# One rotating pool of four PSUM banks for all small TensorE outputs of a four-layer graph attention kernel

## The chip, the cores and the metric

The kernel runs on one core of a Trainium2 chip. The metric is the device time of one execution in microseconds: three runs of the kernel before gave 2642.32, 2642.26 and 2640.95, the median is 2642.26. The profile is one more execution, taken by the hardware profiler; its span is 2639.2 us. Five engines take part: TensorE (PE; its weight loads have a row of their own, PEld), VectorE (DVE), ScalarE (ACT), GpSimd (POOL) and SyncE (SP), which only issues transfers here. Each engine works through its own list of instructions in order, and waits at semaphores for the others.

## What is computed

Sixteen graphs of 1024 nodes with 256 features go through four graph attention layers. All share one adjacency matrix. Layers 0 and 2 have four heads of 64 features, layers 1 and 3 one head of 256. The reference, cut to one layer:

```python
h = jnp.maximum(_layernorm(x, axis=-1), 0.0)
Wh = (h @ W).reshape(B, N, H, D)
e = s_src[:, :, None, :] + s_dst[:, None, :, :]      # two dot products of Wh with a
e = jnp.where(e > 0, e, slope * e)
e = jnp.where(mask, e, -jnp.inf)
alpha = jax.nn.softmax(e, axis=2)
h_out = jnp.einsum('bijh,bjhd->bihd', alpha, Wh)
x = x + jax.nn.elu(h_out)                            # relu in layer 3
```

All inputs and outputs are float32.

## The kernel before

**Steps.** One step is one layer of one graph: 64 steps in all. `order_of_steps` interleaves four graphs ("streams"), so that the next layer of a graph is prepared while steps of other graphs run.

**A step's main part.** `weights` (L335, DVE) makes the unnormalised attention tile `w` of 128 source nodes by 1024 target nodes; there are 18 buffers for such tiles. `aggregate` (L351, PE) multiplies `w` with the projected features `whx` and accumulates over the eight source tiles in a PSUM tile `acc`: for four heads one `acc` holds four target tiles of one head (128 x 260), for one head it holds one target tile (128 x 257). ScalarE copies every `acc` to SBUF (L366). An `acc` tile is done with when this copy has read it.

**A step's ending.** `finish` divides by the softmax sum and applies ELU on DVE, ACT and POOL (L383, L392, L399, L405, L406): only then is the graph's new `x` there.

**The preparation of a later step.** `preparation` takes the statistics of `x` (L222 on DVE, L245 to L257 on POOL), normalises on ACT (`xn`, L263), transposes on PE (L271) and applies ReLU on the way out of PSUM (`hT`, L272). It projects each of the eight node tiles on PE (L282, 128 x 264 or 128 x 258) and copies the result to SBUF on ACT (L284); after every fourth projection two short exponentials follow on ACT (L290, L292), and after the last one two more (`factors`, L300 and L301). `rows` transposes the attention factors on PE (L306), ACT copies them (`gT`, L308), and a transfer through DRAM spreads them over the partitions (`gs`, L324), whence ACT puts them into PSUM (`g`, L330).

**The order.** The order on each engine is the order in which Python emits the pieces: `tc.manual_schedule()` takes it as it is. Between two calls of `aggregate`, `prepare` emits those pieces of later steps whose hand-written due times (`FOUR`, `ONE`, `LATE`, in eighths of a step) have come. So runs of transposes and projections stand between aggregations on PE, and their copies stand in the same order on ACT, between the copies of `acc`.

**PSUM.** [...] `ps_g` holds two tiles of two banks for `g`. `ps_acc` has two banks, for `acc` (and for half of the mask transposes at the start). `ps_p` has two banks, named `pp`, for transposes, projections, rows, and two small things done four times in all (L132, L152). A tile taken from a pool gets a buffer that an earlier tile has left; the first matmul into it waits until the last reader of that earlier tile is through.

Of the kernel before, what the change touches and what calls it, by code (L numbers as in the profile page):

```python
# [14 lines left out]

# [1 line left out]

# [6 lines left out]
F32 = mybir.dt.float32  # L26
BF16 = mybir.dt.bfloat16
# [5 lines left out]
PSUM = bass.MemoryType.PSUM  # L33

P = 128
# [25 lines left out]
def kernel(ctx: ExitStack, tc: tile.TileContext, x, adj, ws, avs, out):  # L61
    nc = tc.nc
    B, N, F = x.shape
    C = N // P
    K = F // P
    HALF = C // 2
# [27 lines left out]
    small = ctx.enter_context(tc.tile_pool(name="small", bufs=4))  # L94
    work = ctx.enter_context(tc.tile_pool(name="work", bufs=2))
    ps_g = ctx.enter_context(tc.tile_pool(name="ps_g", bufs=2, space=PSUM))
    ps_acc = ctx.enter_context(tc.tile_pool(name="ps_acc", bufs=2, space=PSUM))
    dram = ctx.enter_context(tc.tile_pool(name="dram", bufs=4, space=bass.MemoryType.DRAM))
    ps_p = ctx.enter_context(tc.tile_pool(name="ps_p", bufs=2, space=PSUM))

    L = len(LAYERS)
    steps = order_of_steps(B, L)
    xs = {}
    state = [dict() for _ in steps]

    def heads_of(t, H):


        return t[..., 0:F + H].rearrange("p c (h d) -> p c h d", h=H)
# [7 lines left out]
    def weight_columns(l):  # L117

        H, slope, hs, _ = LAYERS[l]
        D = F // H  # L120
        st = {}

        def vectors(queue=nc.sync):

            st["a"] = prep.tile([P, HALF, H, D], F32, name="e")
            queue.dma_start(
                out=st["a"][0:1, 2:4],
                in_=bass.AP(tensor=avs[l].tensor, offset=avs[l].offset,
                            ap=[[0, 1], [D, 2], [hs, H], [1, D]]))

        def spread():
            pa = ps_p.tile([P, 2, H, D], F32, name="pp")  # L132
            nc.tensor.matmul(pa.rearrange("p t h d -> p (t h d)"), lhsT=ones[0:1, :],
                             rhs=st["a"][0:1, 2:4].rearrange("p t h d -> p (t h d)"),
                             start=True, stop=True)
            nc.scalar.activation(st["a"][:, 0:2], pa, AF.Copy)

        def columns():
            for k in range(K):
                for part in range(2):  # L140
                    prod = st["a"][:, 2 + part]
                    wk = heads_of(wx[l], H)[:, k]
                    nc.vector.tensor_mul(prod, wk[:, :, 0:D], st["a"][:, part])
                    nc.vector.tensor_reduce(
                        wk[:, :, D] if part else wx[l][:, k, F + H:F + 2 * H], prod, AX.X, ALU.add)
            st["sq"] = small.tile([P, K, H], F32, name="sq", bufs=1)
            wd = heads_of(wx[l], H)[:, :, :, D]
            nc.vector.tensor_tensor(st["sq"], wd, wd, op=ALU.mult)

        def bound():  # L150

            pn = ps_p.tile([P, H], F32, name="pp")  # L152
            for k in range(K):
                nc.tensor.matmul(pn, lhsT=ones, rhs=st["sq"][:, k, :], start=(k == 0),
                                 stop=(k == K - 1))
            top = small.tile([P, 1], F32, name="top", bufs=1)
            nc.vector.tensor_reduce(top, pn, AX.X, ALU.max)
            nc.gpsimd.tensor_tensor(top, top, half1, op=ALU.pow)
            nc.gpsimd.tensor_scalar(cbias[l], top, 16.01, None, op0=ALU.mult)
            nc.gpsimd.tensor_scalar(nbias[l], top, -16.01 * slope, None, op0=ALU.mult)  # L160
            nc.gpsimd.tensor_scalar(rbias[l], top, -16.01 * (1.0 - slope), SHIFT,
                                    op0=ALU.mult, op1=ALU.add)

        return vectors, spread, columns, bound

    pairs = {}

    def mask_rows(c):

        st = {}  # L170

        def fetch_rows():
            st["raw"] = work.tile([P, N], I32, name="w", bufs=WBUFS)
            nc.sync.dma_start(out=st["raw"], in_=adj.rearrange("(p c) j -> p c j", p=P)[:, c])

        def sign():
            st["sgn"] = work.tile([P, 2, N], BF16, name="w", bufs=WBUFS)
            nc.vector.tensor_scalar(st["sgn"][:, 0], st["raw"], -1.0, 1.0, op0=ALU.max,
                                    op1=ALU.min)

        def turn():

            if c < HALF:
                if c % 2 == 0:
                    pairs[c // 2] = ps_g.tile([P, 2, C, P], BF16, name="g")
                pm = pairs[c // 2][:, c % 2]
            else:
                pm = ps_acc.tile([P, C, P], BF16, name="acc")
            st["pm"] = pm
            sgn = st["sgn"][:, 0].rearrange("p (q c) -> p c q", c=C)  # L190
            for jc in range(C):
                nc.tensor.transpose(pm[:, jc, :], sgn[:, jc, :], identb)

        def positive():
            nc.vector.tensor_scalar(masks[0][:, :, c * P:(c + 1) * P], st["pm"], 0.0, None,
                                    op0=ALU.is_gt)

        def nonzero():
            nc.scalar.activation(masks[1][:, :, c * P:(c + 1) * P], st["pm"], AF.Square)

        return fetch_rows, sign, turn, positive, nonzero

    def load(b, parts=1):
# [6 lines left out]
    def preparation(n):  # L210

        b, l = steps[n]
        H, slope, _, _ = LAYERS[l]
        D = F // H
# [51 lines left out]
        def transpose(half, k):  # L266
            if k == 0:
                st["hT", half] = prep.tile([P, K, HALF * P], F32, name="hT")
            pt = ps_p.tile([P, HALF, P], F32, name="pp")
            for q in range(HALF):  # L270
                nc.tensor.transpose(pt[:, q, :], st["xn", half][:, q, k * P:(k + 1) * P], ident)  # L271
            nc.scalar.activation(st["hT", half][:, k, :], pt.rearrange("p q i -> p (q i)"),  # L272
                                 AF.Relu)

        def project(c):
            if c == 0:
                st["whx"] = prep.tile([P, C, F + 2 * H], F32, name="whx", bufs=3)
                st["rcol"] = small.tile([P, C, H], F32, name="rcol")
            half, q = divmod(c, HALF)
            pw = ps_p.tile([P, F + 2 * H], F32, name="pp")  # L280
            for k in range(K):
                nc.tensor.matmul(pw, lhsT=st["hT", half][:, k, q * P:(q + 1) * P],  # L282
                                 rhs=wx[l][:, k, :], start=(k == 0), stop=(k == K - 1))
            nc.scalar.activation(st["whx"][:, c, :], pw, AF.Copy)  # L284
            if q < HALF - 1:
                return

            s = slice(half * HALF, (half + 1) * HALF)
            wh = heads_of(st["whx"], H)[:, s]
            nc.scalar.activation(st["rcol"][:, s], wh[:, :, :, D], AF.Exp, bias=rbias[l],  # L290
                                 scale=1.0 - slope)
            nc.scalar.activation(wh[:, :, :, D], wh[:, :, :, D], AF.Exp, bias=nbias[l],  # L292
                                 scale=slope)
            nc.gpsimd.tensor_tensor(wh[:, :, :, 0:D], wh[:, :, :, 0:D],  # L294
                                    wh[:, :, :, D:D + 1].to_broadcast([P, HALF, H, D]),
                                    op=ALU.mult)
# [5 lines left out]

        def rows():

            pt = ps_p.tile([C * H, P], F32, name="pp")
            nc.tensor.transpose(pt, st["gcol"].rearrange("p c h -> p (c h)"), ident)  # L306
            gT = small.tile([C * H, P], F32, name="gT", bufs=2)
            nc.scalar.activation(gT, pt, AF.Copy)  # L308
            st["grow"] = dram.tile([H, C, P], F32, name="grow")
            nc.sync.dma_start(out=st["grow"].rearrange("h c i -> c h i"), in_=gT)  # L310

        out = [lambda: stats(0), lambda: stats(1), combine_all, lambda: normalise(0), lambda: normalise(1)]
        for half in range(2):
            out += [lambda half=half, k=k: transpose(half, k) for k in range(K)]
            out += [lambda c=c: project(c) for c in range(half * HALF, (half + 1) * HALF)]


        out += [factors, rows, lambda: fetch_heads(n + 1), lambda: None]
        return [(at, piece) for at, piece in zip(agenda_of[n], out, strict=True)]

# [18 lines left out]
    def aggregate(n, h, i0, per):  # L339
        H = LAYERS[steps[n][1]][0]  # L340
        D = F // H
        st = state[n]
        if h == 0 and i0 == 0:
            st["y"] = work.tile([P, C, H, D + 1], F32, name="y")
        acc = ps_acc.tile([P, per, D + 1], F32, name="acc")
        cols = P // 2 if H > 1 else P
        for q in range(per):
            for jc in range(C):
# [259 lines left out]
```

## Time and profile before

| engine | busy us | share of the span | instructions |
|---|---|---|---|
| PE | 2539.8 | 96% | 40088 |
| PEld | 2256.5 | 86% | 40088 |
| DVE | 2041.7 | 77% | 2144 |
| ACT | 1133.4 | 43% | 2502 |
| POOL | 1021.5 | 39% | 1040 |

The granted TensorE clock was 0.989 of full speed on average. The share of busy time is a mean over the whole span. A PE row in the profile begins with a matmul and ends where the matmul's end is modelled, so two neighbouring rows can overlap: 16 projections take 3.73 us as a row that begins at 1193.83, and the next row begins at 1197.48, only 3.65 us later. The distances between starts are therefore the better clock for PE. In a wait list, "PE pp L282 <- ACT whx L284: 11.2, 27, 3.7" means that the PE matmuls of line 282 were preceded by 11.2 us of idle PE, 27 times, at most 3.7 us at once, and that an ACT instruction of line 284 ended it.

### The profile page before, as it was taken

What the parts mean: (1) busy time and instruction counts of PE and PEld (TensorE: products, weight loads), DVE (VectorE), ACT (ScalarE), POOL (GpSimd) and SP (SyncE); (2) the same over time, 40 slices, a digit from 0 to 9 for tenths busy, and PEclk for the clock granted to TensorE, in tenths of its full rate; (3) what the DMA queues carried; (4) which work ended last, traced back from release to release, by engine and by line L of the source; (5) the groups of instructions that cost most, each with busy time, mean ns of one, the idle gap of its engine ahead of it and who ended that gap; (6) DMA issues with size and microseconds to landing.
All of it is one profiled execution on the core that took longest, in us unless ns stands there. A gap on an engine that the chain in (4) does not pass through costs nothing.

```text
span 2639.2 us, 87794 instructions
## 1 busy us (share of the span) xinstructions
PE 2539.8 (96%) x40088; PEld 2256.5 (86%) x40088; DVE 2041.7 (77%) x2144; ACT 1133.4 (43%) x2502; POOL 1021.5 (39%) x1040
## 2 busy tenths in 40 slices
PE   6899998999999999999999999999999999999899
PEld 4788887888888888888898888888888888888888
DVE  7888566877778877778877778877778877777973
ACT  4343443344444344544344444344444344443341
POOL 2234353423433434443323444433433334444231
PEclk8999999999999999999999999999999999999999
DMA  4101001111112100102211101101112200111101
GB/s 176 51 27 42 26 26 34 42 49 67 50 58 74 42 19 34 42 34 74 74 54 62 42 34 42 42 20 65 50 58 74 74 19 34 42 34 43 51 18 56
DMA packets 36987, 128.98 MB, mean 49 GB/s; under 512 B 6278, under 2 KB 9094, under 8 KB 34696
## 3 DMA queue, kind: packets, MB, share of 16 engines
q1 hardware_dynamic: 36606, 123.36, 13.3%
q8 instruction: 314, 5.14, 0.8%
q14 instruction: 57, 0.47, 0.1%
q10 hardware_dynamic: 10, 0.00, 0.0%
HBM read 105.91 MB, written 17.43 MB: 47 GB/s over the span
## 4 chain that ended last, share of the span: by engine, by line
PE 66%; DVE 17%; POOL 7%; ACT 6%; issue 3%; DMA 0%; DVEq 0%; ACTq 0%
PE acc L351 46%; PE pp L282 15%; DVE w L335 10%; PE pp L271 4%; POOL x L406 3%; DVE e L405 3%; DVE bn L222 2%; ACT xn L263 2%; POOL rstd L251 2%; ACT e L399 1%; DVE e L392 1%; ACT whx L284 1%; ACT rcol L290 0%; ACT gcol L301 0%; ACT whx L292 0%
## 5 line engine op out<-in xcount | busy, mean ns | idle before, releaser
L351 PE MATMUL acc<-whx,w 128*64 128x65 f32 x36864 | 1911.6, 241 | 26.0 <-DVE w L335 20.9
L351 PEld LDWEIGHTS acc<-whx,w 128*64 128x64 f32 x36864 | 1747.2, 145 | 171.6 <-issue 31.2
L335 DVE SCALAR_TENSOR_TENSOR w<-g,rcol,mask 128x1024 f32<-128x1024 f32 x1280 | 1540.6, 1273 | 445.5 <-PE acc L351 387.4
L366 ACT ACTIVATE y<-acc 128x260 f32<-128x260 f32 (+1 forms) x504 | 194.4, 386 | 1097.5 <-PE acc L351 1097.5
L294 POOL TENSOR_TENSOR whx<-whx 128x1024 f32<-128x1024 f32 x128 | 256.4, 2003 | 667.1 <-ACT whx L292 667.1
L282 PE MATMUL pp<-wx,hT 128*128 128x264 f32 (+1 forms) x2048 | 488.6, 390 | 18.8 <-ACT whx L284 11.2
L393 POOL TENSOR_TENSOR y<-y,r 128x1024 f32<-128x1024 f32 x126 | 264.3, 2108 | 618.7 <-DVE e L392 490.8
L282 PEld LDWEIGHTS pp<-wx,hT 128*128 128x128 f32 x2048 | 379.6, 191 | 98.7 <-ACT whx L284 23.5
L406 POOL TENSOR_TENSOR x<-x,e 128x1024 f32<-128x1024 f32 x96 | 238.1, 2486 | 161.0 <-DVE e L405 155.5
L263 ACT ACTIVATE xn<-x,shift,rstd 128x256 f32<-128x256 f32 x512 | 261.3, 590 | 87.9 <-POOL shift L257 85.8
L284 ACT ACTIVATE whx<-pp 128x264 f32<-128x264 f32 (+1 forms) x512 | 195.7, 386 | 236.4 <-PE pp L282 236.1
L222 DVE BATCH_NORM_STATS2 bn<-x 128x6 f32<-128x256 f32 x512 | 175.8, 410 | 58.0 <-POOL x L406 54.6
L405 DVE SCALAR_TENSOR_TENSOR e<-e,y 128x1024 f32<-128x1024 f32 x96 | 175.6, 1839 | 41.7 <-ACT e L399 35.5
L271 PE MATMUL pp<-ident,xn 128*128 128x128 f32 x1024 | 168.6, 284 | 32.1 <-ACT xn L263 28.4
L271 PEld LDWEIGHTS pp<-ident,xn 128*128 128x128 f32 x1024 | 119.3, 141 | 83.2 <-ACT xn L263 53.6
L330 ACT ACTIVATE g<-gs 128x1024 f32<-128x1024 f32 x160 | 163.6, 1024 | 8.1 <-DVE w L335 4.1
L272 ACT ACTIVATE hT<-pp 128x512 f32<-128x512 f32 x256 | 136.8, 585 | 1.9 <-PE pp L271 0.5
L251 POOL TENSOR_TENSOR rstd<-rstd,neghalf 128x8 f32<-128x8 f32 (+1 forms) x65 | 107.0, 1647 | 12.6 <-DVE shift L252 7.6
L399 ACT ACTIVATE e<-e 128x1024 f32<-128x1024 f32 x96 | 100.7, 1049 | 23.9 <-DVE e L392 20.0
L392 DVE SCALAR_TENSOR_TENSOR e<-y,r 128x1024 f32<-128x1024 f32 x64 | 75.5, 1221 | 2.2
L408 DVE SCALAR_TENSOR_TENSOR x<-y,x 128x1024 f32<-128x1024 f32 x30 | 43.3, 1444 | 10.0 <-POOL y L393 10.0
L245 POOL TENSOR_TENSOR dev<-bn 128x8 f32<-128x8 f32 x63 | 13.2, 209 | 89.8 <-DVE bn L222 89.8
(63 smaller groups left out, 401.7 us busy)
## 6 DMA issues: line engine op xcount, KB each, us to landing
gs<-grow SPq DMA_DIRECT2D x160, 512.0 KB
x<-in_x SPq DMA_DIRECT2D x15, 1024.0 KB
out<-x SPq DMA_DIRECT2D x30, 512.0 KB
w<-in_adj SPq DMA_DIRECT2D x8, 512.0 KB
x<-in_x SPq DMA_DIRECT2D x2, 512.0 KB
wx<-in_L_gnn_W SPq DMA_DIRECT2D x8, 128.0 KB
out<-x SPq DMA_DIRECT2D x8, 128.0 KB
grow<-gT SPq DMA_DIRECT2D x32, 16.0 KB
```

Of the source, the lines that this page charges most:

```text
L222: nc.vector.bn_stats(bn[:, c, :], xs[b][:, c, :])
L263: nc.scalar.activation(xn[:, q, :], xs[b][:, c, :], AF.Identity, bias=st["shift"][:, c:c + 1], scale=st["rstd"][:, c:c + 1])
L271: nc.tensor.transpose(pt[:, q, :], st["xn", half][:, q, k * P:(k + 1) * P], ident)
L282: nc.tensor.matmul(pw, lhsT=st["hT", half][:, k, q * P:(q + 1) * P], rhs=wx[l][:, k, :], start=(k == 0), stop=(k == K - 1))
L284: nc.scalar.activation(st["whx"][:, c, :], pw, AF.Copy)
L294: nc.gpsimd.tensor_tensor(wh[:, :, :, 0:D], wh[:, :, :, 0:D], wh[:, :, :, D:D + 1].to_broadcast([P, HALF, H, D]), op=ALU.mult)
L335: nc.vector.scalar_tensor_tensor(w, state[n]["g", h], state[n]["rcol"][:, jc, h:h + 1], masks[LAYERS[steps[n][1]][3]][:, jc, :], op0=ALU.m ...
L351: nc.tensor.matmul(acc[o % P:o % P + cols, q, :], lhsT=st["w", h, jc][:, o:o + cols], rhs=st["whx"][:, jc, h * (D + 1):(h + 1) * (D + 1)], ...
L366: nc.scalar.activation(st["y"][:, i0:i0 + per, h, :], acc, AF.Copy)
L393: nc.gpsimd.tensor_tensor(yh, yh, rb, op=ALU.mult)
L405: nc.vector.scalar_tensor_tensor(e, e, -1.0, yh, op0=ALU.add, op1=ALU.max)
L406: nc.gpsimd.tensor_add(xh, xh, e)
```

## The change

The two pools `ps_acc` and `ps_p`, of two banks each, become one pool `ps` of four banks. Everything that used them takes its tile from there under one name. A helper, `bank`, cuts the wanted shape out of a full bank. No instruction, shape or order of pieces is edited. The purpose is that any kind of tile can use any of the four banks, so that PE can be further ahead of the engines that empty them.

```diff
-    ps_acc = ctx.enter_context(tc.tile_pool(name="ps_acc", bufs=2, space=PSUM))
+    ps = ctx.enter_context(tc.tile_pool(name="ps", bufs=4, space=PSUM))
-    ps_p = ctx.enter_context(tc.tile_pool(name="ps_p", bufs=2, space=PSUM))
...
+    def bank(*shape):
+        t = ps.tile([P, 512], F32, name="bank")
+        n = math.prod(shape)
+        if len(shape) == 1:
+            return t[:, 0:n]
...
-            pa = ps_p.tile([P, 2, H, D], F32, name="pp")
+            pa = bank(2, H, D)
...
-            pn = ps_p.tile([P, H], F32, name="pp")
+            pn = bank(H)
...
-                pm = ps_acc.tile([P, C, P], BF16, name="acc")
+                pm = ps.tile([P, C, P], BF16, name="bank")
...
-            pt = ps_p.tile([P, HALF, P], F32, name="pp")
+            pt = bank(HALF, P)
...
-            pw = ps_p.tile([P, F + 2 * H], F32, name="pp")
+            pw = bank(F + 2 * H)
...
-            pt = ps_p.tile([C * H, P], F32, name="pp")
+            pt = bank(P)[0:C * H]
...
-        acc = ps_acc.tile([P, per, D + 1], F32, name="acc")
+        acc = bank(per, D + 1)
```

More of the change, by code (lines that the diff above doesn't have):

```diff
@@ L18 @@
+import math
 from contextlib import ExitStack
@@ L104 @@
     state = [dict() for _ in steps]
+    def bank(*shape):
[3 more added lines that the diff above has]
+            return t[:, 0:n]
+        names = "abc"[:len(shape)]
+        return t[:, 0:n].rearrange(f"p ({' '.join(names)}) -> p {' '.join(names)}",
+                                   **dict(zip(names, shape)))
     def heads_of(t, H):
```

## The prediction

> **What bounds the kernel now.** I read the busy shares first, then the waits of PE and of its weight loads, then the chain of waits and the timelines of a few cycles. PE is busy 96% of the span, DVE 77%. The chain that ended last is two thirds PE:
>
> ```profile
> PE 66%; DVE 17%; POOL 7%; ACT 6%; issue 3%; DMA 0%; DVEq 0%; ACTq 0%
> ```
>
> The rest is one recurring detour. From about 340 to 2400 us the kernel repeats itself every 79.1 us (two steps; stretches 1001.91 to 1081.09, 1081.09 to 1160.26 and 1160.26 to 1239.32 are 79.18, 79.17 and 79.06 long). In each cycle the chain leaves PE once, for the ending of a step (L405 on DVE, L406 on POOL, statistics, xn on ACT), and comes back at the transposes of line 271. So a cycle is PE-bound for about 64 us, and latency-bound for about 15.
>
> In the PE-bound part, which waits are waits for a bank? A projection or transpose that waits for ACT whx, ACT gT or ACT y waits for a copy out of PSUM whose result it doesn't use: that is a bank. One that waits for ACT xn waits for data. The PE wait list, then that of the weight loads (us in total, times, longest us):
>
> ```profile
> PE pp L271 <- ACT xn L263: 28.4, 77, 8.4
> PE acc L351 <- DVE w L335: 20.9, 25, 5.2
> PE pp L282 <- ACT whx L284: 11.2, 27, 3.7
> PE pp L282 <- ACT gT L308: 7.3, 15, 0.6
> ...
> PE acc L351 <- ACT y L366: 1.0, 1, 1.0
> ```
> ```profile
> PEld pp L282 <- ACT whx L284: 23.5, 30, 4.1
> ...
> PEld pp L271 <- ACT whx L284: 17.5, 63, 0.3
> PEld pp L282 <- ACT gT L308: 13.6, 15, 1.0
> ```
>
> Bank waits are 11.2 + 7.3 + 1.0 = 19.5 us of idle PE, but 23.5 + 17.5 + 13.6 = 54.6 us (with 2.2 more at acc, 56.8) of idle weight loads. The truth lies between, and starts tell it. The PE timeline of one cycle:
>
> ```profile
> 1009.48 1.29 PE L271 MATMUL pp<-ident,xn 128*128 128x128 f32 x8
> 1010.61 3.64 PE L351 MATMUL acc<-whx,w 128*128 128x257 f32 x16
> 1014.08 1.03 PE L271 MATMUL pp<-ident,xn 128*128 128x128 f32 x8
> 1015.05 3.95 PE L351 MATMUL acc<-whx,w 128*64 128x65 f32 x128
> 1018.93 5.54 PE L282 MATMUL pp<-wx,hT 128*128 128x258 f32 x24
> 1024.64 2.05 PE L282 MATMUL pp<-wx,hT 128*128 128x264 f32 x8 [0.17 <-ACT whx L284]
> 1026.52 1.30 PE L271 MATMUL pp<-ident,xn 128*128 128x128 f32 x8
> ```
>
> The same eight transposes show 1.29 and 1.30 us after projections, but 1.03 after an accumulation. The page calls PE busy there; 0.26 us is lost each time.
>
> [...] rows overlap their successors (3.73 us long, next start after 3.65), which is how a stall stays hidden in a busy row. [...] the 63 + 30 + 15 waits above show where two are short. [...]
>
> **The change, part by part.** In the two built programs the lists of DVE, ACT, POOL and SP are the same, instruction for instruction, with waits for the same engines. PE's list has the same matmuls in the same order; only its waits differ. Before, 676 of 1352 reuses of a bank come after two tiles and 271 after three. After, 1338 of 1352 come after exactly four.
>
> *Can four shared banks be worse than two and two?* Among any five tiles in a row, three are of one kind, so under the old rule the first of these must be emptied before the last begins. Evacuations come in the order of the tiles (ACT is in order), so the oldest of the five is empty then too. The new rule asks for nothing earlier, save where DVE reads a tile too (the masks at the start, line 157, the last step). I laid the new assignment over the old times: every tile's new predecessor had been emptied at least 0.58 us before the tile began, in the steady cycles at least 1.31 us. Before, the margin at a stall is 0.05. So the added waits (an accumulator now also waits for a projection's copy, with all of PE queued behind it, and DVE waiting for PE to release w) should already be met when they are reached.
>
> *What is removed,* start to start:
> - (a) Second transpose tile after projections: 1009.48 to 1010.61 is 1.13 us for eight transposes; the chain of waits gives the unstalled eight at 1014 as 0.87. Loss 0.26, times 63: 16.4.
> - (b) Third 264-column projection, held while ACT runs L290, L292, L300, L301: 1018.93 to 1026.52 is 7.59 for eight tiles. Unstalled, four tiles take 3.65 (1193.83 to 1197.48) and 3.49 (768.57 to 772.06). Loss 0.45, times 26: 11.7.
> - (c) Second projection after rows, held by gT behind a 1.05 us exponential (L399): 1035.48 to 1039.88 is 4.40 against 3.65, loss 0.75, times 15: 11.3.
> - (d) Two long stalls at 166 and 2497 us: 3.27 and 3.74 idle, 7.5 with the restart.
> - (e) One accumulator at 425 us: 1.2.
>
> Sum 48.1.
>
> *What of it counts.* The latency-bound part starts from DVE, which runs without a real gap from 1030.93 to 1067.5, and began when PE released a w buffer:
>
> ```profile
> 1030.93 7.24 DVE L335 SCALAR_TENSOR_TENSOR w<-g,rcol,mask 128x1024 f32<-128x1024 f32 x6 [10.00 <-PE acc L351]
> ...
> 1043.07 16.77 DVE L335 SCALAR_TENSOR_TENSOR w<-g,rcol,mask 128x1024 f32<-128x1024 f32 x14 [0.21 <-PE acc L351]
> ...
> 1067.50 3.29 DVE L405 SCALAR_TENSOR_TENSOR e<-e,y 128x1024 f32<-128x1024 f32 x1 [0.22 <-ACT e L399]
> ```
>
> Both (a) and (b) lie before that release, so they shorten the whole cycle: 2 x 0.26 + 0.45 = 0.97, times 26 cycles: 25.2. Stall (c), at 1037, lies beside this DVE stretch. Of its 0.75 only the two waits inside it, 0.21 + 0.22 = 0.43, can be saved; the rest returns as a longer wait for xn. Times 14 steady cycles: 6.0. In (d), PE gets two projections further (2 x 0.87 = 1.75) and then meets the same late ACT: 2 x 1.75 = 3.5. (e) is whole: 1.2. Outside the cycles remain 11 x 0.26 and one (c), 3.6; DVE ends several waits there, so I take half: 1.8. Sum 37.7.
>
> *What is added:* 32 semaphore instructions on PE, 31 of them at the transposes. The source view has such rows at 51 ns, so 0 to 1.6 us; many stand where PE waits for xn anyway. I take 0.8. Moving a matmul to another bank costs nothing that a row shows: the copies stay 386 ns.
>
> 2642.3 - 37.7 + 0.8 = 2605.
>
> **The rivals.**
> - *All 48.1 us are saved:* DVE is not co-critical, (c) and (d) count whole. 2642.3 - 48.1 = 2594. Against it: the 0.21 and 0.22 above.
> - *The xn wait takes the place:* PE already waits 28.4 us for xn, and if DVE's start hangs on something else than PE, the detour keeps its place in time. Half of the gain stays: 2642.3 - 19 = 2623. Against it: DVE waits 10.00 us for PE right before that stretch.
> - *Slower:* the copies on ACT come in bursts (xn takes 4.05 us in one piece), and a shared pool lets one late copy stop accumulations too. If the margins were an illusion and each of 30 cycles had two new stalls like (a), with nothing gained: 2642.3 + 30 x 0.52 + 1.6 = 2660. Against it: the argument with five tiles, and margins over 1.3 us.
>
> **Chances.** Forecast 0.70, all saved 0.11, half 0.12, nothing 0.02, slower 0.05. The forecast itself is open by some 10 us (how much of (c), (d) and the edges counts). The range from 2590 to 2624 holds it and both neighbours for the most part. Faster by over 0.2%: 0.93; within 0.2%: 0.02; slower: 0.05.
>
> **What would show it.** Right: no PE or PEld wait at L282 and L271 (their new line numbers are 10 higher) for whx or gT worth over 5 us in all; all runs of eight transposes 1.03 us long unless they wait for xn; cycles of about 78.2 us without, and 77.8 with, a gT stall before; the xn wait of PE grown by some 5 us; DVE, ACT and POOL busy times unchanged. Wrong: the same waits under another name (ACT y, say), or cycles that stay at 79.1 us with a longer wait for xn, or a wait of PE for DVE w in the cycles.

## The result and the profile after

| kernel | median us | of the kernel before | 95% interval |
|---|---|---|---|
| before (4 runs) | 2641.61 | | |
| one pool of four banks (4 runs) | 2597.71 | 0.9836 | 0.9819 to 0.9853 |

The kernel before has one run more here than in the text above, 2639.95. The forecast was 2605, with a range from 2590 to 2624; the kernel came out 7 us below the forecast. PE is now busy for 2509.0 us instead of 2539.8, though it runs the same 40088 matmuls. Of the 30.8 us that went, 26.6 went at transposes (168.6 to 155.9 us) and projections (492.8 to 478.9): stalls drawn as busy rows. The rest went mostly at the accumulations; the clock was at half for 51.2 us instead of 60.9, which shortens rows too (at 273 us, 100 matmuls took 4.71 us with most of them at half clock before, and 3.14 at full clock after). Idle PE fell from 99.4 to 87.0 us, only 12.4 of the 43.2 us of shorter span.

The wait list of PE after the change (lines stand 10 higher than before):

```profile
PE bank L281 <- ACT xn L273: 32.3, 92, 9.7
PE bank L361 <- DVE w L345: 21.4, 24, 5.2
...
PE bank L361 <- ACT whx L294: 3.0, 1, 3.0
...
PE bank L292 <- ACT whx L294: 1.8, 1, 1.8
```

Of the bank waits (11.2 for whx, 7.3 for gT, 1.0 for y) two single ones are left, 4.8 us together. The wait for xn, which is data, grew from 28.4 to 32.3.

The list of the weight loads wants care. Before:

```profile
PEld acc L351 <- issue: 31.2, 115, 1.0
```

After:

```profile
PEld bank L361 <- issue: 15.6, 50, 1.7
PEld bank L361 <- ACT whx L294: 13.7, 31, 3.4
...
PEld bank L361 <- ACT rcol L300: 5.5, 33, 0.2
```

This looks like a new bank wait at the accumulators. It is mostly an old gap with a new name. When tiles of 128 columns are followed by tiles of 64, the first weight load waits 0.17 us after transposes and 0.35 after projections, in either kernel. An accumulator now carries a wait for a projection's copy, and the profile puts the gap down to it. Starts show that nothing was added: from the last transpose to the first matmul of 64 columns it is 203 ns before and 202 after, 94 more than between two transposes (109).

The PE timeline of the same piece of a cycle as in the prediction:

```profile
1001.80 7.32 PE L292 MATMUL bank<-wx,hT 128*128 128x258 f32 x32
1008.96 1.04 PE L281 MATMUL bank<-ident,xn 128*128 128x128 f32 x8
```

Eight projections run through in 7.16 us from start to start instead of 7.59 (1018.93 to 1026.52), with no gap between the 258-column and the 264-column ones (the row names the first form). A projection is four matmuls in these rows: the "16 projections" that the section on the profile before reads from a row are 16 matmuls, four projections. The eight transposes after them last 1.04 us instead of 1.30.

Since PE's list holds the same matmuls in the same order, its starts can be subtracted one by one. The changed kernel is ahead by 6.1 us at 340 us of the old time, by 8.4 at 450, by 38.9 at 2349 and by 43.2 at the end. In between it gains 0.96 us in a cycle that had no gT stall, and 1.54 in a cycle that had one. Between 451 and 2454 us neither trace has a stretch at half clock, so the clock has no part in these gains.

The chain that ended last, by engine:

```profile
PE 59%; DVE 25%; POOL 9%; issue 4%; ACT 3%; DMA 0%; DVEq 0%; ACTq 0%
```

PE's share fell from 66 to 59%, DVE's and POOL's rose. PE's part of each cycle became shorter, and the detour to xn hardly did.

### The profile page after: what moved, and what is told of

Same layout as the page of the kernel before. It is cut to its first block, busy times and chain, and to the rows that moved or that the text cites. A ratio compares the mean times of both kernels' runs of the same rounds, so it can differ in the third digit from the quotient of the medians.

```text
span 2596.0 us, 87826 instructions
## 1 busy us (share of the span) xinstructions
PE 2509.0 (97%) x40088; PEld 2258.4 (87%) x40088; DVE 2020.0 (78%) x2144; ACT 1131.7 (44%) x2502; POOL 1035.8 (40%) x1040
## 4 chain that ended last, share of the span: by engine, by line
PE 59%; DVE 25%; POOL 9%; issue 4%; ACT 3%; DMA 0%; DVEq 0%; ACTq 0%
PE bank L361 37%; PE bank L292 17%; DVE w L345 16%; POOL x L416 5%; PE bank L281 4%; DVE bn L232 4%; ACT xn L273 2%; DVE e L415 2%; DVE e L402 2%; POOL rstd L261 2%; ACT e L409 0%; PE bank L316 0%; POOL rstd L259 0%; POOL shift L267 0%; DVE r L393 0%
## 5 line engine op out<-in xcount | busy, mean ns | idle before, releaser
L361 PE MATMUL bank<-whx,w 128*64 128x65 f32 x36864 | 1907.1, 241 | 29.4 <-DVE w L345 21.4
L361 PEld LDWEIGHTS bank<-whx,w 128*64 128x64 f32 x36864 | 1744.0, 144 | 173.4 <-DVE w L345 19.6
L376 ACT ACTIVATE y<-bank 128x260 f32<-128x260 f32 (+1 forms) x504 | 194.2, 385 | 1079.3 <-PE bank L361 1079.3
L292 PE MATMUL bank<-wx,hT 128*128 128x264 f32 (+1 forms) x2048 | 474.9, 386 | 2.0 <-ACT whx L294 1.8
L292 PEld LDWEIGHTS bank<-wx,hT 128*128 128x128 f32 x2048 | 383.7, 190 | 64.4 <-ACT whx L294 2.2
L294 ACT ACTIVATE whx<-bank 128x264 f32<-128x264 f32 (+1 forms) x512 | 194.7, 386 | 209.1 <-PE bank L292 208.7
L281 PE MATMUL bank<-ident,xn 128*128 128x128 f32 x1024 | 155.9, 282 | 32.6 <-ACT xn L273 32.3
L281 PEld LDWEIGHTS bank<-ident,xn 128*128 128x128 f32 x1024 | 120.5, 142 | 70.1 <-ACT xn L273 59.2
L415 DVE SCALAR_TENSOR_TENSOR e<-e,y 128x1024 f32<-128x1024 f32 x96 | 154.2, 1625 | 30.6 <-ACT e L409 17.6
L282 ACT ACTIVATE hT<-bank 128x512 f32<-128x512 f32 x256 | 136.6, 584 | 1.9 <-PE bank L281 0.5
```

What stands on the lines that cost most here:

```text
L361: nc.tensor.matmul(acc[o % P:o % P + cols, q, :], lhsT=st["w", h, jc][:, o:o + cols], rhs=st["whx"][:, jc, h * (D + 1):(h + 1) * (D + 1)], ...
L376: nc.scalar.activation(st["y"][:, i0:i0 + per, h, :], acc, AF.Copy)
L415: nc.vector.scalar_tensor_tensor(e, e, -1.0, yh, op0=ALU.add, op1=ALU.max)
```

## Experiments

### Each stall alone, with two pools

The kernel before keeps its pools of two and two banks. One tile at a time is moved from `ps_p` to `ps_acc`, where an older tile has long been emptied. That takes away one kind of stall. Only edit (c) brings something in its place: four short waits of PE more for an accumulator's copy (ACT y), 1.3 us in all.

(c), rows of one-head steps:

```diff
-            pt = ps_p.tile([C * H, P], F32, name="pp")
+            pt = (ps_acc if H == 1 else ps_p).tile([C * H, P], F32, name="acc" if H == 1 else "pp")
```

> The kernel before (two and two banks), with one edit: the small transpose of rows in one-head steps takes its tile from the accumulators' pool. That removes stall (c) alone, 15 times 0.75 us, 11.3 in all. Theory (a stall counts where nothing else is in its way; DVE runs beside this one and gives only part): the cycles that had this stall shrink from 79.18 to about 78.6, 2642 becomes about 2633. Rival A (every stall on PE counts whole): those cycles shrink by 0.75 to 78.43, about 2630. Rival B (the gain comes from accumulators having more banks, not from these stalls): nothing, 2642.

(a), the second transpose tile of second halves:

```diff
-            pt = ps_p.tile([P, HALF, P], F32, name="pp")
+            pt = (ps_acc if (half, k) == (1, 1) else ps_p).tile(
+                [P, HALF, P], F32, name="acc" if (half, k) == (1, 1) else "pp")
```

> The kernel before, with one edit: the second transpose tile of the second half takes its tile from the accumulators' pool. That removes stall (a) alone, 63 times 0.26 us, 16.4 in all. Theory: all of it lies before DVE is released, so every cycle shrinks by 0.52; about 2626. The runs of eight transposes after projections should last 1.03 us instead of 1.30. Rival B (gain from more accumulator banks): 2642. Rival C (the transposes' 0.26 us is only how rows are drawn, no time): 2642, with the rows shorter all the same.

(b), the third projection of four-head steps:

```diff
-            pw = ps_p.tile([P, F + 2 * H], F32, name="pp")
+            pw = (ps_acc if H > 1 and c == 2 else ps_p).tile(
+                [P, F + 2 * H], F32, name="acc" if H > 1 and c == 2 else "pp")
```

> The kernel before, with one edit: the third projection of a four-head step takes its tile from the accumulators' pool. That removes stall (b) alone, 26 times 0.44 us, 11.4 in all. Theory: all of it lies before DVE is released, so every cycle shrinks by 0.44; about 2630. Rival B (gain from more accumulator banks): 2642.

All three edits together:

> The kernel before, still with two and two banks, and the three edits together: the rows of one-head steps, the second transpose tile of second halves, and the third projection of four-head steps take accumulators' banks. Stalls (a), (b), (c) are gone; the two long ones (d) at 166 and 2497 us and the one accumulator (e) at 425 us stay. Theory: cycles of 77.6 and 78.1 us, as with the shared pool; time about 2605, that is all of the gain but the 7 or 8 us at the start and the end. Rival B: 2642. Rival D (sharing as such brings something that no named stall explains): clearly more than 2610.

| edit | median us | against before (2641.59) | 95% interval of the ratio |
|---|---|---|---|
| (c) | 2633.09 | -8.5 | 0.9954 to 0.9979 |
| (a) | 2626.34 | -15.3 | 0.9922 to 0.9949 |
| (b) | 2632.10 | -9.5 | 0.9946 to 0.9971 |
| all three | 2606.81 | -34.8 | 0.9853 to 0.9880 |

The three parts add up to 33.3, and together they give 34.8. With two pools of two banks, the three named stalls account for 34.8 of the 43.9 us. Rival B (accumulators with more banks) expected nothing and fails, and so does D. In a cycle with a gT stall, (c) alone gains 0.56 to 0.61 us and not 0.75: rival A fails too. Nearly every cycle gains 0.51 to 0.54 from (a) and 0.43 to 0.45 from (b), whole as counted.

Rival C of the second test is answered by the timeline of the kernel with edit (a) (its line numbers are one higher):

```profile
1003.24 0.60 PE L272 MATMUL pp<-ident,xn 128*128 128x128 f32 x4
1003.67 0.60 PE L272 MATMUL acc<-ident,xn 128*128 128x128 f32 x4
1004.11 3.64 PE L352 MATMUL acc<-whx,w 128*128 128x257 f32 x16
```

The eight transposes take 0.87 us from start to start, where the kernel before took 1.13, and the execution is shorter by as much each time. The 0.26 us, invisible as idle PE, were time.

Against the shared pool 9.1 us are missing (9.9 between the two profiled executions). By starts, 3.3 of them lie before 450 us, around the first long stall of (d) and (e), which were left out. Another 3.3 lie after 2319, where the second long stall itself gives nothing, and stay open. Most of the rest is one pause that the profile puts down to issue and that no edit explains:

```profile
1195.87 10.66 PE L353 MATMUL acc<-whx,w 128*64 128x65 f32 x247 [2.81 <-issue]
```

### Three shared banks

```diff
-    ps = ctx.enter_context(tc.tile_pool(name="ps", bufs=4, space=PSUM))
+    ps = ctx.enter_context(tc.tile_pool(name="ps", bufs=3, space=PSUM))
```

> The changed kernel with three banks in the shared pool instead of four. Theory: what matters is how many tiles come between two uses of a bank. At three, the stalls (a), (b), (c) stay away, but an accumulator right after the transposes that wait for xn has to wait for the copy of the accumulator before them, which stands behind 4.05 us of xn on ACT: on the old times it would begin 1.58 us too early, in 29 of the 35 places where a tile would begin too early. About 1.7 us each with the restart: about 50 to 58 us more than with four, 2650. Rival (sharing is what counts, three banks are enough): 2600 to 2608.

Measured: 2685.33, a ratio of 1.0160 (1.0144 to 1.0176). Sharing as such is not what counts: with three banks the kernel is slower than with two separate pairs. The wait list of PE names the expected stall:

```profile
PE bank L361 <- ACT y L376: 49.2, 34, 2.4
```

That is the expected place, and 34 times instead of 29. Start to start most of them are 1.63 us; all together they make 54.9, and some 58 with 0.1 us each for the restart (the second matmul after a stall comes 0.1 us late once more: in the kernel before 321 to 327 ns behind the first, where 216 to 222 are usual for these 257 to 264 columns). That is what was expected. But the kernel lost 88 against four banks: the expected 2650 was too low. The rest is seen in stretches just after such a stall (us from the span's start; length, busy time of PE, PEld, DVE, ACT, POOL; then the granted PE clock):

```profile
1012.00:1017.00 5.00, 3.04 (x15) 1.89 (x14) 5.00 (x5) 4.55 (x10) 3.83 (x12) 1.00 0.00 0
1017.00:1021.00 4.00, 4.00 (x12) 3.19 (x12) 3.05 (x3) 2.68 (x6) 0.00 (x0) 0.57 0.00 0
```

The granted clock was 0.57 over the second stretch, which is half clock for about 3.4 of its 4 us. The trace's clock record has 112.6 us at half clock before 2560 us with three banks, 47.8 with four (mean granted clock 0.978 and 0.991). If PE is the bound there, 64.8 us at half clock are up to 32 us lost: with the 58 us that is a little more than the whole loss. This sum is an estimate.

### Three banks and one

```diff
-    ps_acc = ctx.enter_context(tc.tile_pool(name="ps_acc", bufs=2, space=PSUM))
+    ps_acc = ctx.enter_context(tc.tile_pool(name="ps_acc", bufs=1, space=PSUM))
...
-    ps_p = ctx.enter_context(tc.tile_pool(name="ps_p", bufs=2, space=PSUM))
+    ps_p = ctx.enter_context(tc.tile_pool(name="ps_p", bufs=3, space=PSUM))
...
-                pm = ps_acc.tile([P, C, P], BF16, name="acc")
+                pm = (ps_p if c % 2 else ps_acc).tile([P, C, P], BF16, name="pp" if c % 2 else "acc")
```

> Separate pools, three banks for projections, transposes and rows and one for accumulators (half of the mask tiles at the start go to the larger pool, so that the start doesn't lock up). Theory: stalls (a) to (c) are gone, but each of 377 accumulators that follow another one directly waits for its copy, 0.69 us each on the old times and some 0.1 to restart, up to 300 us less what DVE's part hides: 2800 to 2900. Rival (the projections' side alone needed banks): 2605.

Measured: 2796.12, ratio 1.0579 (1.0565 to 1.0594). It lies just below the range given.

```profile
PE acc L351 <- ACT y L366: 154.4, 309, 3.2
```

Of these 309 waits, 268 stand right after another accumulator, where 377 were expected. So neither division by kind serves: two banks are too few for runs of projections, one is too few for runs of accumulators. Three for accumulators and one for the rest was not run. One pool lends the banks to whoever runs. Two pools come within 9 us of it only with the tiles assigned one by one, as above.

### Later transposes, with one pool and with two

The wait for xn is what is left. In these two kernels PE has one more accumulation to do before it needs xn.

```diff
-FOUR = (-8, -8, -5, -3, -2, -1, -1, 0, 0, 0, 0, 0, 0, 2, 2, 2, 2, 3, 8, 8, 10)
-ONE = (2, 2, 2, 4, 4, 5, 5, 6, 6, 6, 6, 6, 6, 8, 8, 8, 8, 8, 10, 10, 12)
+FOUR = (-8, -8, -5, -2, -1, -1, -1, 0, 0, 0, 0, 0, 0, 2, 2, 2, 2, 3, 8, 8, 10)
+ONE = (2, 2, 2, 4, 4, 6, 6, 7, 7, 7, 7, 7, 7, 8, 8, 8, 8, 8, 10, 10, 12)
```

> The changed kernel with other due times: in one-head steps the transposes of the first half come one eighth of a step later (6 instead of 5) and the projections of the first half and transposes of the second at 7 instead of 6; in four-head steps the normalisations come one eighth later (-2 and -1), so that the buffers follow. PE then has one more accumulation (3.5 us) to do before it needs xn. Theory: what still holds the cycle at 77.6 or 78.1 us is the detour over DVE, POOL and ACT to xn; 1.15 to 1.6 us of PE wait per cycle go, 2598 becomes about 2565. Rival (the wait comes up again elsewhere, at w or at a projection): 2590 to 2600.

> The kernel before (two and two banks) with the same later due times. Theory: the wait for xn goes, 1.0 to 1.5 us per cycle, and the bank stalls stay: about 2612. Then every bank stall is on the path, and between this kernel and the one with the shared pool and the same due times there lies the full 48 us that I counted, not 44. Rival (the two waits are one: whichever is removed, the other takes its place): 2635 to 2642.

With one pool: 2567.90, ratio 0.9716 (0.9703 to 0.9730), the fastest of all kernels here. The chain that ended last is PE's nearly throughout:

```profile
PE 89%; DVE 7%; ACT 1%; issue 1%; POOL 1%; DMA 0%; DVEq 0%; ACTq 0%
```

The detour was what held the cycle.

With two pools: 2630.02, ratio 0.9951 (0.9938 to 0.9963), where 2612 was expected. The wait for xn went, but the later due times put four transpose tiles in a row, and with two banks the third waits for the first one's copy. The PE timeline of that kernel:

```profile
1004.64 1.29 PE L271 MATMUL pp<-ident,xn 128*128 128x128 f32 x8
1006.42 1.14 PE L271 MATMUL pp<-ident,xn 128*128 128x128 f32 x8 [0.49 <-ACT hT L272]
```

From start to start this new stall is 0.66 us, 26 times, 17 us. It accounts for the miss: 62 us lie between the two late kernels, and 48 from the stalls counted in the prediction and 17 from the new one give 65. Neither rival fits: the two waits are not one. With four shared banks the same sixteen transposes run without a break:

```profile
1061.39 1.91 PE L281 MATMUL bank<-ident,xn 128*128 128x128 f32 x16
```

### Three shared banks and later transposes

The edit to three banks again, on the late kernel.

> The kernel with the late transposes, with three shared banks instead of four. It tells apart why three banks cost 88 us with the early transposes: there 34 waits of 1.6 us stood right after the wait for xn, and 16 more stretches of 3.4 us at half the TensorE clock came with them. Here, on the times of four banks, 75 tiles per run would begin 0.43 us too early (the second pair of transposes, in a row of four) and the long stall behind xn is gone. Theory: about 0.55 us each with the restart, some 40 us more than with four, about 2610, and no more stretches at half clock than the 8 there are with four banks. Rival (three banks bring the halved clock whatever the length of the stalls): 2640 or more.

Measured: 2592.67, ratio 0.9811 (0.9794 to 0.9827), 25 us above four banks. The sign and the order were right, the 40 us too much. The 75 tiles that would start early come three to a cycle, but only one stall per cycle is seen:

```profile
PE bank L281 <- ACT hT L282: 8.2, 26, 0.3
```

It probably pushes the other two tiles back too. Starts show 0.48 us for it (0.54 with the restart), 26 times, 14 us. Of the other 11, most lies in the edges: by starts 5.3 us are lost before 460 us and 5.5 after 2300, and what they are stays open. The clock record has 8 stretches at half clock before 2560 us, as the late kernel with four banks has; two of them are longer, 64.9 us in all against 58.0 (mean granted clock 0.987 and 0.988), which can be up to 3.5 us of the loss at the edges, an estimate. Between 460 and 2300 us neither has one (granted clock 1.00 in both). So here three banks don't bring the halved clock by themselves, and the rival fails.

## Why the prediction was right, point by point

- **Stalls hide in busy rows.** Shown by the test of (a) alone, and by 26.6 us less busy PE for the same transposes and projections. Of the three measures, idle PE (19.5 us) was far too low and idle weight loads (56.8) too high; starts gave 48.1.
- **(a) and (b) shorten every cycle.** Forecast 0.97 a cycle, measured 0.96.
- **(c) counts in part.** Forecast 0.43, measured 0.58. Right in kind, too small in size. The step that was mis-sized took only DVE's two waits. The chain also held the second L405, whose 3.29 us are shown in the prediction (the median of the 96 is 1.24). It ran beside an addition on POOL that had started just before it:

```profile
1067.36 2.35 POOL L406 TENSOR_TENSOR x<-x,e 128x1024 f32<-128x1024 f32 x1 [1.16 <-DVE e L405]
1070.86 2.36 POOL L406 TENSOR_TENSOR x<-x,e 128x1024 f32<-128x1024 f32 x1 [1.16 <-DVE e L405]
```

  After the change, ACT no longer delays it, and both of these DVE instructions take 3.30 together; then POOL does its two additions in one piece:

```profile
1013.11 7.25 DVE L345 SCALAR_TENSOR_TENSOR w<-g,rcol,mask 128x1024 f32<-128x1024 f32 x6 [9.29 <-PE bank L361]
...
1047.00 3.30 DVE L415 SCALAR_TENSOR_TENSOR e<-e,y 128x1024 f32<-128x1024 f32 x2
```
```profile
1049.24 5.58 POOL L416 TENSOR_TENSOR x<-x,e 128x1024 f32<-128x1024 f32 x2 [1.16 <-DVE e L415]
```

  From DVE's release to the end of POOL's second addition it is 1030.93 to 1073.22, 42.29 us, before, and 1013.11 to 1054.82, 41.71, after: the 0.58 us. POOL's two additions end this piece in either kernel. So one forecast sign failed: the busy times of DVE and POOL were to stay, but DVE's fell from 2041.7 to 2020.0 us (L405 alone from 175.6 to 154.2), and POOL's rose from 1021.5 to 1035.8.
- **The steady cycles.** Forecast 25.2 + 6.0 = 31.2 us; between 450 and 2349 us the kernel gained 30.5. The 26 cycles of the forecast were 24 in that stretch; the larger (c) made up for it.
- **The two long stalls (d).** Forecast 1.75 us each, 3.5 together; that the two gave about 3 is luck. At 166 us the gain was 3.4, because a second effect went with the stall (see below). At the other nothing was gained: the changed kernel is ahead by 42.9 us just before the old stall and by 42.5 at 2523 us of the old time. Before:

```profile
2497.22 2.72 PE L282 MATMUL pp<-wx,hT 128*128 128x258 f32 x8 [3.74 <-ACT whx L284]
```

  After, PE got two projections further as said, and then an accumulator had to wait, which in two pools it would not have:

```profile
2455.32 8.94 PE L361 MATMUL bank<-whx,w 128*64 128x65 f32 x256 [2.96 <-ACT whx L294]
```

  This is the one place where the added wait is seen to act. It is where ACT stood still for 4.81 us behind DVE.
- **The edges.** Forecast 3.5 + 1.2 + 1.8 = 6.5 us; measured 8.4 before 450 us and 4.3 after 2349, 12.7. Here lies nearly all of the 7 us between the forecast and the result. Of it, 1.6 us came at 273 us, where a stretch at half clock fell away that had no bank wait before it (see below).
- **The added waits are met when they are reached.** Right but for the case above. The 32 added semaphore instructions, priced at 0.8 us, can't be told apart here.
- **The rivals.** By its total alone the result lies nearer to "all saved" (2594) than to the forecast; only the parts tell them apart. "All saved" fails on (c), with 0.58 of 0.75 us, and on the second long stall; "half saved" fails on the cycles, "slower" on the margins; three banks show that "slower" was no idle thought, and that the margin belongs to four.

## What to carry to other kernels

Ask of each PSUM tile how many tiles come between two uses of its bank, and whether the engine that empties it can be that far behind; a shared pool turns fixed borders into that one number, and here four was enough and three was not. Measure stalls of PE from start to start, since idle time showed 19.5 us where 48 were lost. When the buffer waits are gone, look for the next latency chain: here later due times for a few steps brought a further 30 us (2597.7 to 2567.9).

## What was not expected

At 166 us a stall of PE cost more than its length. Before, around that stall (PE, PEld, DVE, ACT, POOL; then the granted PE clock):

```profile
164.30:167.00 2.70, 0.79 (x4) 0.71 (x5) 2.70 (x3) 1.61 (x3) 2.13 (x1) 1.00 0.01 3
167.00:170.30 3.30, 3.30 (x9) 2.57 (x8) 3.30 (x3) 1.36 (x5) 2.55 (x2) 0.51 0.00 0
```

After:

```profile
164.30:167.00 2.70, 0.92 (x4) 0.65 (x4) 2.70 (x3) 2.09 (x5) 2.05 (x1) 1.00 0.01 3
167.00:170.30 3.30, 3.30 (x19) 2.80 (x18) 3.30 (x3) 2.25 (x9) 3.30 (x3) 1.00 0.00 0
```

Before, after 3.27 us of idle PE, the granted clock was 0.51 over the next 3.3 us and PE ran 9 matmuls. After the change, with 1.78 us idle, the clock was 1.00 and PE ran 19. The clock record has 3.4 us at half clock here; the 1.7 us that they can cost are an estimate, and make up the other half of the gain at this place.

At 273 us the same thing happened without any bank wait. In both kernels PE waits three times for w there (0.47, 0.85 and 0.86 us before; 0.49, 0.86 and 0.85 after). What follows is at a granted clock of 0.50 before (first line), and of 1.00 after the change (second line):

```profile
272.90:276.30 3.40, 3.40 (x70) 3.40 (x67) 3.40 (x4) 0.00 (x0) 0.00 (x0) 0.50 0.02 5
```
```profile
268.90:272.30 3.40, 3.40 (x95) 3.25 (x91) 3.40 (x4) 0.39 (x1) 0.00 (x0) 1.00 0.02 5
```

With three banks it happened in some cycles and not in others, after the same waits of 0.16 and 1.47 us at most. Here it did (granted clock 0.57 from 1017 to 1021 us), and the 16 matmuls of the last line take 5.42 us; 81 us later they take 3.74 (granted clock 1.00 from 1097 to 1101 us):

```profile
1013.10 0.33 PE L281 MATMUL bank<-ident,xn 128*128 128x128 f32 x1
...
1014.57 0.76 PE L281 MATMUL bank<-ident,xn 128*128 128x128 f32 x5 [0.16 <-ACT xn L273]
1016.81 5.42 PE L361 MATMUL bank<-whx,w 128*128 128x257 f32 x16 [1.47 <-ACT y L376]
```

So a stall of 1.47 us cost more than itself in one of these two cycles and not in the other. What decides between the two is not shown by these runs.
